# A Toeplitz convolution on TensorE: the zero quarter of each 128x128 tile is left out, with 64x64 tiles for the first halves of chunks and the states, and 128x64 tiles for the second halves

## The chip, the cores and the metric

The kernel runs on one core of a Trainium2 chip. The metric is device time in microseconds (us) of one execution. Names in the text are those of the profile: PE is TensorE's matmuls, PEld its weight loads, DVE is VectorE, ACT is ScalarE, POOL is GpSimd, SP is SyncE, which issues most transfers. L760 is line 760 of the kernel before.

## The reference

The model takes x (64 batches, 64 heads, 1024 positions), runs a masked long convolution per head, and adds a feed-forward layer that is a mixture of 64 experts of rank 16.

```python
mask = (jnp.arange(Lq) < length[:, None]).astype(u.dtype)
u_m = u * mask[:, None, :]
kernel = _get_kernel(log_dt, C, log_A_real, A_imag, Lq)   # K = 2 Re sum_n Cs exp(dtA * l)
n = 2 * Lq
k_f = jnp.fft.rfft(kernel, n=n)
u_f = jnp.fft.rfft(u_m, n=n)
y = jnp.fft.irfft(u_f * k_f, n=n)[..., :Lq]
y = y + u_m * D[:, None]
cond = y * mask[:, None, :]
...
scores = xf @ Wr.T
top_vals, top_idx = jax.lax.top_k(scores, TOPK)
gates = jax.nn.softmax(top_vals, axis=-1)
...
h = jnp.einsum('nd,krd->nkr', xf, A)
out = jnp.einsum('nkr,kdr->nd', h * G[:, :, None], B)
x = x + (out * SCALING).reshape(*prefix, -1)
```

All of it is in 32-bit floats. The convolution of a head is causal: position l of the output takes the positions up to l, with a kernel that is a sum of 64 decaying complex exponentials.

## The kernel before

A sequence of 1024 positions is cut into 8 chunks of 128. Within a chunk the convolution is a product with a 128x128 triangular Toeplitz matrix (`toep`, one per head); what comes from earlier chunks goes through 64 complex states per head. The 64 heads are worked in 8 groups g of 8 heads, a group in 4 pairs i of two heads hh. The work of a group on TensorE is, in order:

- `into_states` (L696 to L712, called by `begin`): per pair and per real or imaginary part c, two products of x with the tables `bt` into the bank `pu`, one head into PSUM partitions 0 to 63 and the other into 64 to 127 (128x64 tiles, 448 columns: 7 chunks of 64 batches). ScalarE copies the bank to the states `s`.
- `recur`: VectorE runs the recurrence over the chunks on `s` (scalar_tensor_tensor, L465 by the helper).
- `inside` (L751, matmul at L760): per head, the Toeplitz tile times x: 128 rows, 128 columns of weights, 512 columns of x (8 chunks of 64 batches) into a bank `pc`.
- `across` (L765, matmul at L769): per pair, per c and per head, 64 state rows times the table `w`, added to columns 64 on of the same bank (64x128 tiles, 448 columns). The head picks the row half of the array.
- L777: VectorE multiplies each `pc` with the mask into `y`, the feature layout that the layer behind reads.

A group runs `inside(0), inside(1), across(0), across(1)` (the names `first_two`), later `inside(2), inside(3), across(2), across(3)` (`last_two`). Between and around them `conv` yields, and products of the group before (L652, the first factor of the experts, by Strassen's seven products at 128x128 with 256 columns) are put in. After `last_two` comes `begin(g + 1)` with the next group's `into_states`, then the gates (`psh`, L849). In group 0 there is little to put in between. The second factor (L1172) runs after the last group, from 606.7 us to the end.

Each 32-bit matmul call is two records of PE and two of PEld in the profile, except transposes. PSUM: `pc` and `pu` share the banks of `ps_k` and `ps_c`, two each, by pair. So the first `pu` after `last_two` needs the bank of pair 2 to be freed by its mask product.

x of a pair (512 KB) is loaded by SyncE (`load_x`, L147) into one of four tiles; the tile is free when `inside` of its last user is done. The Toeplitz tiles are made through DRAM: the first 128 values of each head's kernel (plus D at place 0) are stored to `krows` behind 127 zeros, and one transfer with overlapping rows reads them as a 128x128 tile per head (`rows_by_head`, L333 and L334; `rows` for group 0, L340 and L342). The tables of groups 0 to 3 are made from powers `lv`, those of groups 4 to 7 in transposed form by `tables_as_they_lie`. A planner orders instructions of an engine by the order of the program unless they are not ready in its estimate; where the order is pinned, the code says `keep_in_program_order`.

Of the kernel before, what the change touches and what calls it, by code (L numbers as in the profile page):

```python
# [37 lines left out]
F32 = mybir.dt.float32  # L38
# [6 lines left out]
P = 128  # L45
# [19 lines left out]
NW = P + 1  # L65
# [15 lines left out]
def constants():  # L81


    c = np.zeros((P, NW + P + 2 + NBLK), np.float32)
    c[:, :NW] = np.arange(NW)
    c[:, NW : NW + P] = np.eye(P)
    for hh in range(2):
        c[hh * NS : (hh + 1) * NS, NW + P + hh] = 1.0
    c[:, NW + P + 2 :] = P * np.arange(NBLK)[None, :] + np.arange(P)[:, None]
    return c  # L90


def body(ctx: ExitStack, tc, x, xo, lens, par, dvec, dgrp, at, bm, wt, cst, out):
# [34 lines left out]
    cst_sb = ids.tile([P, NW + P + 2 + NBLK], F32, tag="cst", name="cst_sb")  # L128
# [3 lines left out]
    d_sb = const.tile([2, NP], F32, tag="dvec", name="d_sb")  # L132
    nc.scalar.dma_start(d_sb, dvec)
    d_of_group = const.tile([HG, NG], F32, tag="dgrp", name="d_of_group")
# [4 lines left out]
    feat = cst_sb[:, NW + P + 2 :]  # L139
# [115 lines left out]
    def tables(g):  # L255
# [62 lines left out]
        def kernels_by_vector():  # L318

            kc = tabp.tile([P, HG], F32, tag="kc", name=f"kc_{g}")  # L320
            V.tensor_reduce(kc.rearrange("p (i a) -> p i a", a=2),
# [3 lines left out]
            ks = tabp.tile([HG, P], F32, tag="ks8", name=f"ks8_{g}")  # L325
            nc.scalar.copy(ks, pk)
            return ks

        def rows_by_head(ks):

            tt(ks[:, 0:1], ks[:, 0:1], d_of_group[:, g : g + 1], ALU.add)
            row = krows[h0 : h0 + 1, :]
            nc.sync.dma_start(krows[h0 : h0 + HG, P - 1 :], ks)  # L333
            nc.sync.dma_start(toep, bass.AP(row.tensor, row.offset, [[1, P], [KROW, HG], [1, P]]))  # L334

        def rows(ks, i, n):

            tt(ks[:, :, 0], ks[:, :, 0], d_sb[:, j0 + i : j0 + n], ALU.add)
            row = krows[h0 + 2 * i : h0 + 2 * i + 1, :]
            nc.sync.dma_start(  # L340
                krows[h0 + 2 * i : h0 + 2 * n, P - 1 :].rearrange("(i a) l -> a i l", a=2), ks)
            nc.sync.dma_start(toep[:, 2 * i : 2 * n, :],  # L342
                              bass.AP(row.tensor, row.offset, [[1, P], [KROW, 2 * (n - i)], [1, P]]))

        def tables_as_they_lie():
# [7 lines left out]

            mag, f, lo, k = (flat(t) for t in ("mag", "f", "sn", "k"))
            place = feat[:, 0:1]
# [4 lines left out]
            nc.scalar.activation(mag, mag, AF.Exp, scale=place)  # L360
            ts(f, f, place, ALU.mult)
# [3 lines left out]
            stt(f, lo, place, ALU.mult, f, ALU.add)  # L365
# [41 lines left out]
        for i in range(GP if g < DIRECT else 0):  # L407
            j = j0 + i
            re, im = w[:, 0, i, :P], w[:, 1, i, :P]
# [3 lines left out]
            b = bb[:, i % 2]  # L413
            for c, by in enumerate((alpha, nbeta)):
                if g == 0:
                    ts(b[:, c, :], re, by[:, j : j + 1], ALU.mult)
                else:
                    nc.scalar.activation(b[:, c, :], re, AF.Copy, scale=by[:, j : j + 1])
            stt(b[:, 0, :], im, nbeta[:, j : j + 1], ALU.mult, b[:, 0, :], ALU.add)
            stt(b[:, 1, :], im, nalpha[:, j : j + 1], ALU.mult, b[:, 1, :], ALU.add)  # L420
# [16 lines left out]
        V.tensor_copy(turn[:, 0:2], w[:, :, :, P])  # L437
# [286 lines left out]

    def conv(g, steps, out):
# [13 lines left out]
        def recur(*pairs):  # L739
            for k in range(1, NCH):  # L740
                for i in pairs:
                    s, a = states[i][1], turn[:, 0, i : i + 1]
                    stt(s[:, :, k, :], s[:, :, k - 1, :], a, ALU.mult, s[:, :, k, :], ALU.add)
                for i in pairs:
                    s, b = states[i][1], turn[:, 1, i : i + 1]
                    stt(s[:, 0, k, :], s[:, 1, k - 1, :], b, ALU.mult, s[:, 0, k, :], ALU.add)
                for i in pairs:
                    s, nb = states[i][1], turn[:, 2, i : i + 1]
                    stt(s[:, 1, k, :], s[:, 0, k - 1, :], nb, ALU.mult, s[:, 1, k, :], ALU.add)

        def inside(i):  # L751
            xt, s = states.pop(i)
            pcs = []
            for hh in range(2):
# [653 lines left out]
```

## Time and profile before

| | |
|---|---|
| time, median of 3 runs | 951.28 us (951.0 to 951.71) |
| profiled execution, first to last instruction | 949.7 us; a time of its own is not listed, and 1.6 us lie between it and the median |
| PE busy | 937.7 us (99%), 4232 records |
| PEld busy | 724.9 us |
| DVE busy | 735.8 us (77%) |
| POOL busy | 332.1 us (35%) |
| ACT busy | 160.5 us (17%) |
| inside (L760) | 128 records, 57.7 us of PE |
| across (L769) | 256 records, 53.8 us of PE |
| into the states (L707) | 256 records, 50.5 us of PE |

A row of a group of instructions gives line, engine, operation, output <- input, partitions x elements of both, count, then busy time in us and the mean duration of one in ns, then the idle time of the engine just before them and what ended it. The ends of matmuls are modelled and overlap the next one, so the sum of durations is more than the busy time. A row of the timeline begins with the start and the length of a merged stretch in us from the span's start; in a stretch table a line gives the stretch, its length, the busy time asked for, the TensorE clock granted (1.00 is full speed), the share of the 16 DMA engines' time in use and GB/s.

### The profile page before, as it was taken

The numbers are of one execution on the slowest core, as the hardware profiler recorded it, in microseconds if no ns is written. First come the engines' busy times: TensorE is split into PE (matmuls) and PEld (weight loads), VectorE is DVE, ScalarE is ACT, GpSimd is POOL, SyncE is SP. The second block draws the span as 40 slices with busy tenths as digits, with TensorE's granted clock in tenths as the row PEclk, the third lists the DMA queues.
The fourth block names the chain that finished last, engine by engine and source line by source line (L and its number), as shares of the span: only waits on it lengthen the run. The fifth ranks groups of instructions, "written<-read, shape, count | busy, mean of one in ns | idle before, by whom it ended". The sixth has DMA issues, their size and how long they took to land. (4 is left out here: it accounts for less than half of the span.)

```text
span 949.7 us, 11906 instructions
## 1 busy us (share of the span) xinstructions
PE 937.7 (99%) x4232; PEld 724.9 (76%) x4232; DVE 735.8 (77%) x1717; ACT 160.5 (17%) x292; POOL 332.1 (35%) x285
## 2 busy tenths in 40 slices
PE   7999999999999999999999999999999999999998
PEld 2476767587587587587587688888888888888887
DVE  8899798697995995995893498869856865785674
ACT  5343233312402402411210000000000000000000
POOL 0203204043042041041142032256745554764565
PEclk9999999999999999999999999999999999999999
DMA  8815325237444434334332374663682575258332
GB/s 289 220 44 179 106 85 170 101 102 215 123 127 167 122 119 162 136 108 157 118 106 89 127 253 164 217 236 107 218 283 88 177 263 180 92 208 306 103 123 100
DMA packets 72043, 149.32 MB, mean 157 GB/s; under 512 B 9808, under 2 KB 20784, under 8 KB 71984
## 3 DMA queue, kind: packets, MB, share of 16 engines
q1 hardware_dynamic: 52300, 99.65, 31.8%
q0 software_dynamic: 16864, 47.22, 15.3%
q10 hardware_dynamic: 2820, 1.69, 0.6%
q8 instruction: 33, 0.54, 0.2%
q14 instruction: 26, 0.21, 0.1%
HBM read 100.13 MB, written 47.33 MB: 155 GB/s over the span
## 5 line engine op out<-in xcount | busy, mean ns | idle before, releaser
L465 DVE SCALAR_TENSOR_TENSOR s<-s,turn 128x64 f32<-128x64 f32 (+1 forms) x432 | 119.4, 324 | 2.7 <-ACT s L712 2.0
L652 PE MATMUL h<-y,waa 128*128 128x256 f32 x512 | 117.9, 381 | 0.0
L652 PE MATMUL h<-y,was 128*128 128x256 f32 x512 | 116.5, 380 | 0.0
L652 PE MATMUL h<-ty,was 128*128 128x256 f32 x512 | 116.0, 380 | 0.0
L934 POOL TENSOR_TENSOR hg<-h_p,gx 128x512 f32<-128x512 f32 x16 | 26.8, 1678 | 242.8 <-DVE h_p L465 238.1
L652 PEld LDWEIGHTS h<-y,waa 128*128 128x128 f32 x512 | 96.2, 190 | 19.0 <-issue 6.5
L652 PEld LDWEIGHTS h<-y,was 128*128 128x128 f32 x512 | 97.0, 190 | 14.8 <-issue 1.5
L652 PEld LDWEIGHTS h<-ty,was 128*128 128x128 f32 x512 | 97.3, 190 | 13.7 <-DVE f L465 0.8
L934 POOL TENSOR_TENSOR hg<-h_u,gx 128x512 f32<-128x512 f32 x32 | 48.6, 1519 | 74.5 <-DVE h_u L454 48.3
L1186 ACT COPY p<-s 128x512 f32<-128x512 f32 x28 | 16.4, 586 | 312.4 <-PE s L1172 312.4
L1031 POOL TENSOR_TENSOR o<-o,acc_a 128x512 f32<-128x512 f32 x32 | 47.6, 1506 | 41.4 <-DMA r<-hg_dram 21.7
L652 PE MATMUL h<-ty,waa 128*128 128x256 f32 x256 | 58.4, 382 | 0.0
L760 PE MATMUL pc<-x,toep 128*128 128x512 f32 x128 | 57.7, 594 | 0.6 <-DVE y L777 0.6
L777 DVE TENSOR_TENSOR y<-pc,mask 128x512 f32<-128x512 f32 x64 | 40.7, 682 | 21.4 <-PE pc L769 21.3
L652 PEld LDWEIGHTS h<-ty,waa 128*128 128x128 f32 x256 | 48.3, 190 | 9.5 <-issue 2.0
L454 DVE TENSOR_TENSOR o<-o,s 128x512 f32<-128x512 f32 x50 | 34.1, 682 | 23.5 <-PE s L1172 17.9
L1031 POOL TENSOR_TENSOR o<-o,b_room 128x512 f32<-128x512 f32 x32 | 48.7, 1542 | 9.8 <-DVE b_room L454 9.8
L907 POOL DMA_DIRECT2D gx<-gt_dram x56 | 33.8, 618 | 50.9 <-DMA gt_dram<-gt 50.9
L707 PE MATMUL pu<-x,bt 128*64 128x448 f32 x256 | 50.5, 544 | 0.0
L937 POOL DMA_DIRECT2D hg_dram<-hg x32 | 25.6, 801 | 69.5 <-DVE hg L454 44.5
L1031 POOL TENSOR_TENSOR o<-o,u 128x512 f32<-128x512 f32 x36 | 45.8, 1298 | 10.0 <-DVE u L454 9.7
L454 DVE TENSOR_TENSOR hg<-hg 128x512 f32<-128x512 f32 x64 | 42.4, 681 | 4.7 <-POOL hg L934 4.3
(270 smaller groups left out, 1645.6 us busy)
## 6 DMA issues: line engine op xcount, KB each, us to landing
x<-in_x SPq DMA_DIRECT2D x32, 512.0 KB
hg_dram<-hg POOLq DMA_DIRECT2D x16, 1024.0 KB, 6.0
o<-in_xo SPq DMA_DIRECT2D x64, 256.0 KB
out<-o SPq DMA_DIRECT2D x63, 256.0 KB
gx<-gt_dram POOLq DMA_DIRECT2D x56, 256.0 KB, 4.9
qy<-hg_dram SPq DMA_DIRECT2D x28, 512.0 KB
r<-hg_dram SPq DMA_DIRECT2D x26, 512.0 KB
hg_dram<-hg POOLq DMA_DIRECT2D x16, 768.0 KB, 4.2
```

The lines of the kernel that those rows point to most:

```text
L454: V.tensor_tensor(out=o, in0=a, in1=b, op=o_)
L465: V.scalar_tensor_tensor(out=o, in0=a, scalar=s, in1=b, op0=o1, op1=o2)
L652: nc.tensor.matmul(bank[:, ii, :], lhsT=fac[n - 1][:, k, (j + ii) * P : (j + ii + 1) * P], rhs=rf[n - 1][:, k, :], start=(first and ii == ...
L707: nc.tensor.matmul(pu[hh * NS : (hh + 1) * NS, :], lhsT=bt[:, i, (1 - c) * P + hh * NS : (1 - c) * P + (hh + 1) * NS], rhs=xt[:, hh, : NCH ...
L760: nc.tensor.matmul(pc, lhsT=toep[:, 2 * i + hh, :], rhs=xt[:, hh, :], start=True, stop=False)
L777: marks["y"] = V.tensor_tensor(out=y[:, :, i // 2, 2 * (i % 2) + hh, :], in0=pcs[hh].rearrange("p (k b) -> p k b", b=NB), in1=mask, op=ALU ...
L907: i = queue.dma_start(gx[:, ii, :], gt_dram[g, c * n : (c + 1) * n, :].unsqueeze(1).to_broadcast([n, RANK, TOK]),)
L934: G.tensor_tensor(out=o, in0=a, in1=b, op=op)
L937: nc.gpsimd.dma_start(hg_dram[g, :, a:b, j : j + 2, :], hg[:, a:b])
L1031: tc.keep_in_program_order(G.tensor_tensor(out=o, in0=a, in1=b, op=op_))
L1186: nc.scalar.copy(p1, c11)
```

## The change

A lower triangular 128x128 tile has a 64x64 quarter that is zero. The change doesn't multiply it:

- The first 64 outputs of a chunk come from its first 64 inputs alone (`early_halves`): 64x64 tiles with 256 columns, 4 chunks at a time. The last 64 come from all 128 inputs (`late_halves`): 128x64 tiles with 256 columns.
- The head hh of a pair now picks the row half in which the first 64 inputs lie: x and the Toeplitz tiles of the even heads have their two halves exchanged. The even chunks (e = 0) and the odd chunks (e = 1) are put apart in x, in the states and in the banks, and the odd chunks' outputs have their halves exchanged (`half_of`), so that the four early products of a pair lie on four different 64x64 quarters of the array.
- `across` is also cut into 64x64 tiles: per pair, c and e, four products with the same four quarters; 192 columns for e = 0 (its first chunk has no state before it) and 256 for e = 1. So there are 16 calls per pair instead of 4.
- The order becomes `early_halves` of two pairs, `across` of both, `late_halves` of both. The mask product and the release of the x tile stand behind the late halves.
- The rows of the Toeplitz tile go through three stores and three loads instead of one and one, and D is added at a place that depends on the head.
- The tables get two segments of 65 powers, in an order that depends on the head (131 columns instead of 129), and the transposed tables of groups 4 to 7 do three of their operations per head half. The mask's positions, x, A and Wr are permuted on their way in, to the new order of y's features.

```diff
-NW = P + 1
+HP = P // 2
+SEG = HP + 1
+NW = 2 * SEG + 1
...
+    c = np.zeros((P, NW + P + 2 + NBLK + 1), np.float32)
+    for hh in range(2):
+        for seg in range(2):
+            late = seg == hh
+            c[hh * NS : (hh + 1) * NS, seg * SEG : (seg + 1) * SEG] = HP * late + np.arange(SEG)
+    c[:, NW - 1] = P
...
+def places():
+
+
+    t, p = np.arange(NBLK)[None, :], np.arange(P)[:, None]
+    odd = t // KH
+    return P * (2 * (t % KH) + odd) + (p + HP * odd) % P
...
+        def load_toeplitz(i, n):
+
+
+            row = krows[h0 + 2 * i : h0 + 2 * i + 1, :]
+            heads_of = toep[:, 2 * i : 2 * n, :].rearrange("p (i a) c -> p a i c", a=2)
+
+            def load(o, count, start):
+                nc.sync.dma_start(
+                    o, bass.AP(row.tensor, row.offset + start, [[1, count], [2 * KROW, n - i], [1, P]]))
+
+            load(heads_of[:, 1], P, KROW)
+            load(heads_of[:HP, 0], HP, HP)
+            load(heads_of[HP:, 0], HP, 0)
+
         def rows_by_head(ks):
 
-            tt(ks[:, 0:1], ks[:, 0:1], d_of_group[:, g : g + 1], ALU.add)
-            row = krows[h0 : h0 + 1, :]
-            nc.sync.dma_start(krows[h0 : h0 + HG, P - 1 :], ks)
-            nc.sync.dma_start(toep, bass.AP(row.tensor, row.offset, [[1, P], [KROW, HG], [1, P]]))
+            first = ks.rearrange("h (s j) -> h s j", s=2)[:, :, 0]
+            tt(first, first, d_of_group[:, g, :], ALU.add)
+            dst = krows[h0 : h0 + HG, P - 1 :].rearrange("(i a) l -> a i l", a=2)
+            nc.sync.dma_start(dst[1], ks[GP:])
+            nc.sync.dma_start(dst[0, :, HP:], ks[:GP, :HP])
+            nc.sync.dma_start(dst[0, :, :HP], ks[:GP, HP:])
+            load_toeplitz(0, GP)
...
+            def of_heads(t, hh):
+                return t.rearrange("p (i a n) -> p a i n", a=2, n=NS)[:, hh]
+
             mag, f, lo, k = (flat(t) for t in ("mag", "f", "sn", "k"))
-            place = feat[:, 0:1]
             row(f, 1)
             row(mag, 0)
             row(lo, 2)
             yield
-            nc.scalar.activation(mag, mag, AF.Exp, scale=place)
-            ts(f, f, place, ALU.mult)
+            for hh in range(2):
+                nc.scalar.activation(of_heads(mag, hh), of_heads(mag, hh), AF.Exp, scale=place_of[hh])
+            for hh in range(2):
+                ts(of_heads(f, hh), of_heads(f, hh), place_of[hh], ALU.mult)
             ts(k, f, MAGIC, ALU.add, MAGIC, ALU.subtract)
             yield
             tt(f, f, k, ALU.subtract)
-            stt(f, lo, place, ALU.mult, f, ALU.add)
+            for hh in range(2):
+                stt(of_heads(f, hh), of_heads(lo, hh), place_of[hh], ALU.mult, of_heads(f, hh), ALU.add)
...
         for i in range(GP if g < DIRECT else 0):
             j = j0 + i
-            re, im = w[:, 0, i, :P], w[:, 1, i, :P]
+            re, im = (w[:, c, i, : 2 * SEG].rearrange("p (s j) -> p s j", s=2)[:, :, :HP]
+                      for c in range(2))
...
+    def of_chunk(k):
+
+        return k // 2 + KH * (k % 2)
+
...
         def recur(*pairs):
             for k in range(1, NCH):
+                now, was = of_chunk(k), of_chunk(k - 1)
                 for i in pairs:
                     s, a = states[i][1], turn[:, 0, i : i + 1]
-                    stt(s[:, :, k, :], s[:, :, k - 1, :], a, ALU.mult, s[:, :, k, :], ALU.add)
+                    stt(s[:, :, now, :], s[:, :, was, :], a, ALU.mult, s[:, :, now, :], ALU.add)
                 for i in pairs:
                     s, b = states[i][1], turn[:, 1, i : i + 1]
-                    stt(s[:, 0, k, :], s[:, 1, k - 1, :], b, ALU.mult, s[:, 0, k, :], ALU.add)
+                    stt(s[:, 0, now, :], s[:, 1, was, :], b, ALU.mult, s[:, 0, now, :], ALU.add)
                 for i in pairs:
                     s, nb = states[i][1], turn[:, 2, i : i + 1]
-                    stt(s[:, 1, k, :], s[:, 0, k - 1, :], nb, ALU.mult, s[:, 1, k, :], ALU.add)
...
-        def inside(i):
-            xt, s = states.pop(i)
-            pcs = []
-            for hh in range(2):
-                if g == 0:
-                    banks, tag = ((ps_c, "pc"), (ps_f, "pf"))[i % 2]
-                else:
-                    banks, tag = ((ps_k, "pk"), (ps_c, "pc"))[i % 2]
-                pc = banks.tile([P, NBLK * NB], F32, tag=tag, name=f"pc_{g}_{i}_{hh}")
-                nc.tensor.matmul(pc, lhsT=toep[:, 2 * i + hh, :], rhs=xt[:, hh, :],
-                                 start=True, stop=False)
-                pcs.append(pc)
-            return i, s, pcs
-
-        def across(i, s, pcs, pinned=False):
+                    stt(s[:, 1, now, :], s[:, 0, was, :], nb, ALU.mult, s[:, 1, now, :], ALU.add)
+
+        def half_of(e, late):
+
+            c = (e ^ late) * HP
+            return slice(c, c + HP)
+
+        def chunks(e):
+            return slice(e * KH * NB, (e + 1) * KH * NB)
+
+        def early_halves(*pairs):
+
+
+            made = []
+            for i in pairs:
+                xt, s = states.pop(i)
+                pcs = []
+                for hh in range(2):
+                    if g == 0:
+                        banks, tag = ((ps_c, "pc"), (ps_f, "pf"))[i % 2]
+                    else:
+                        banks, tag = ((ps_k, "pk"), (ps_c, "pc"))[i % 2]
+                    pcs.append(banks.tile([P, NBLK * NB], F32, tag=tag, name=f"pc_{g}_{i}_{hh}"))
+                for e in range(2):
+                    for hh in range(2):
+                        r = slice(hh * HP, (hh + 1) * HP)
+                        nc.tensor.matmul(
+                            pcs[hh][half_of(e, 0), chunks(e)], lhsT=toep[r, 2 * i + hh, :HP],
+                            rhs=xt[r, hh, chunks(e)], start=True, stop=False, skip_group_check=True)
+                made.append((i, xt, s, pcs))
+            return made
+
+        def across(i, xt, s, pcs, pinned=False):
             for c in range(2):
+                for e in range(2):
+                    into, of = ((slice(NB, KH * NB), slice(KH, NCH)), (chunks(1), slice(0, KH)))[e]
+                    for hh in range(2):
+                        o = hh * NS
+                        for late in range(2):
+                            seg = SEG * (hh if late else 1 - hh) + 1
+                            m = nc.tensor.matmul(
+                                pcs[hh][half_of(e, late), into], lhsT=w[o : o + NS, c, i, seg : seg + HP],
+                                rhs=s[o : o + NS, c, of].rearrange("p k b -> p (k b)"),
+                                start=False, stop=False, skip_group_check=True,
+                            )
+                            if pinned:
+                                tc.keep_in_program_order(m)
+
+        def late_halves(i, xt, s, pcs):
+            for e in range(2):
                 for hh in range(2):
-                    o = hh * NS
-                    m = nc.tensor.matmul(
-                        pcs[hh][:, NB:], lhsT=w[o : o + NS, c, i, 1:],
-                        rhs=s[o : o + NS, c].rearrange("p k b -> p (k b)"),
-                        start=False, stop=(c == 1),
-                    )
-                    if pinned:
-                        tc.keep_in_program_order(m)
+                    nc.tensor.matmul(
+                        pcs[hh][half_of(e, 1), chunks(e)], lhsT=toep[:, 2 * i + hh, HP:],
+                        rhs=xt[:, hh, chunks(e)], start=False, stop=(e == 1), skip_group_check=True)
             for hh in range(2):
                 marks["y"] = V.tensor_tensor(
                     out=y[:, :, i // 2, 2 * (i % 2) + hh, :],
...
-        first_two = inside(0), inside(1)
+        first_two = early_halves(0, 1)
         across(*first_two[0])
         across(*first_two[1])
+        late_halves(*first_two[0])
+        late_halves(*first_two[1])
...
-        last_two = inside(2), inside(3)
+        last_two = early_halves(2, 3)
         across(*last_two[0])
         across(*last_two[1])
+        late_halves(*last_two[0])
+        late_halves(*last_two[1])
         step(1)
         if g + 1 < NG:
             begin(g + 1)
...
+    turned = np.concatenate([xr[:, HP:], xr[:, :HP]], 1)
+    xc = np.where((np.arange(NH) % 2 == 0)[:, None, None, None], turned, xr)
+    xc = xc.reshape(NH, P, KH, 2, NB).transpose(0, 1, 3, 2, 4)
+    dh = np.zeros((2, NP, 2), np.float32)
+    for hh in range(2):
+        dh[hh, :, 1 - hh] = D.reshape(NP, 2)[:, hh]
+    place = places()
     arrays = {
-        "x": xr.reshape(NH, P, NBLK * NB),
+        "x": xc.reshape(NH, P, NBLK * NB),
 
...
-        "at": A.reshape(NE * RANK, NBLK, P).transpose(2, 1, 0),
+        "dvec": dh,
+        "dgrp": dh.reshape(2, NG, GP, 2).transpose(0, 2, 1, 3).reshape(HG, NG, 2),
+        "at": A.reshape(NE * RANK, L).T[place],
...
-        "wt": Wr.reshape(NE, NBLK, P).transpose(2, 1, 0),
+        "wt": Wr.T[place],
```

## The prediction

> **What bounds the kernel now.** First the busy shares, then the chain of waits:
>
> ```profile
> PE 937.7 (99%) x4232; PEld 724.9 (76%) x4232; DVE 735.8 (77%) x1717; ACT 160.5 (17%) x292; POOL 332.1 (35%) x285
> ...
> PE s L1172 35%; PE h L652 7%; PE psh L849 0%; PE last L1172 0%; DVE ey L1007 0%; DVE acc_a L454 0%; PE psc L859 0%; DVE o L454 0%; DVE e L990 0%; DVEq L454 0%
> ```
>
> TensorE is busy for 937.7 of 949.7 us, and almost all of the rest is the start, where it waits for loads. Every other engine has a fifth of its time free or more. So a microsecond taken from TensorE is a microsecond of the kernel, as long as nothing that TensorE then reaches sooner is late. The groups of TensorE instructions say how much lies in the part that changes:
>
> ```profile
> L760 PE MATMUL pc<-x,toep 128*128 128x512 f32 x128 | 57.7, 594 | 0.6 <-DVE y L777 0.6
> L769 PE MATMUL pc<-s,w 64*128 64x448 f32 x192 | 40.4, 554 | 0.0
> L769 PE MATMUL pc<-s_more,w 64*128 64x448 f32 x64 | 13.4, 537 | 0.0
> ```
>
> That is 57.7 us inside the chunks and 53.8 out of the states. Each call leaves two records (64 calls, 128 records), one after the other on the same tile of the array. The mean duration of a record overlaps with its neighbours, so prices come from the distance between starts. The timeline of TensorE around the second half of one group's convolution:
>
> ```profile
> 302.64 3.62 PE L652 MATMUL h<-y,was 128*128 128x256 f32 x16
> 306.09 3.62 PE L652 MATMUL h<-y,waa 128*128 128x256 f32 x16
> ...
> 313.00 3.60 PE L760 MATMUL pc<-x,toep 128*128 128x512 f32 x8
> 316.52 1.78 PE L769 MATMUL pc<-s,w 64*128 64x448 f32 x8
> 318.13 1.67 PE L769 MATMUL pc<-s_more,w 64*128 64x448 f32 x8
> 319.73 6.24 PE L707 MATMUL pu<-x,bt 128*64 128x448 f32 x32
> ```
>
> Sixteen records of 256 columns take 3.45 us: 0.216 us for a pass of 256 columns over the whole array. The weight loads of the same stretch show what half tiles do:
>
> ```profile
> 316.52 0.30 PEld L769 LDWEIGHTS pc<-s,w 64*128 64x128 f32 x4 [0.76 <-issue]
> 317.00 0.20 PEld L769 LDWEIGHTS pc<-s,w 64*128 64x128 f32 x2 [0.18 <-issue]
> 317.38 0.19 PEld L769 LDWEIGHTS pc<-s,w 64*128 64x128 f32 x2 [0.18 <-issue]
> 317.75 0.19 PEld L769 LDWEIGHTS pc<-s_more,w 64*128 64x128 f32 x2 [0.18 <-issue]
> ```
>
> They come two at a time, a pair each 0.375 us, so the two row halves run side by side at 448 columns. L707 does the same with column halves: 32 records in 6.06 us, 0.375 a pair and 0.06 at the start. By length, 192 columns take 0.162.
>
> **What a change of tile shape costs.** The last L760 start is at 316.00 and L769 starts at 316.52: 0.09 more than the 0.43 between 512-column records. L769's first pair then takes 0.48 instead of 0.375, another 0.10 while the 128-column weights come in; on going to 64-column weights this is 0.05 (L707: 319.73 to 320.16).
>
> **The change on TensorE, for two head pairs** (half of a group's convolution; `first_two` or `last_two`).
> Before: 8 records of 0.431 inside, 8 pairs of 0.375 across: 3.45 + 3.00 = 6.45 us. Shape changes: in and out of 64x128, 0.38 where products (128x128) follow, 0.34 where L707 (128x64) follows. 6.83 and 6.79.
> After, if four 64x64 tiles run at once: early halves, two records on each of four tiles per pair of heads, 2 x 2 x 0.216 = 0.86. Across, per pair and per c two rounds of 192 and two of 256 columns: 2 x 0.162 + 2 x 0.216 = 0.755, x 4 = 3.02; the same work as before in four times the instructions. Late halves, four records on each of two column tiles per pair: 2 x 4 x 0.216 = 1.72. Sum 5.60. Changes of shape: into 64x64 0.14, into 128x64 0.14, back to 128x128 0.19; but L707 follows the late halves in the same shape and costs nothing. 6.07 and 5.88.
> So the first half of a group gains 0.76 us and the second 0.91: 1.67 a group, 11.7 us over groups 1 to 7.
>
> The trace has no four tiles at once. Its bounds are the rows with two: all four (both the row halves of L769 and the column halves of L707 show no loss) or only two. I take four, since each pair of the four is one of these two combinations. In the late halves the second column tile's work stands behind four records of the first, where the trace shows it passing two; if it can pass no more, one pass of 0.216 is lost per half, 3.0 us in all. I take 0 and keep 3.0 for the range.
>
> That the tiles run ahead of each other is seen at the head of the stage. The two records of a call stand one behind the other for one tile, and the second of one tile has to wait 0.375 us for the first; still two start before 316.8, so one of them is the other head's:
>
> ```profile
> 316.52 0.65 PE L769 MATMUL pc<-s,w 64*128 64x448 f32 x2
> ```
>
> [...]
>
> **What comes earlier and may be late.**
> (1) x. A tile of x is free only after its late half, no more after L760. SyncE's queue shows the two loads of 512 KB for the next group:
>
> ```profile
> 314.91 2.09 SPq L147 DMA_DIRECT2D x<-in_x  x2
> ```
>
> They are issued at 1.92 and 3.63 us after the half's start at 313.00, 0.2 after their L760 records. After the change, pair 2's late half ends at 0.14 + 0.86 + 3.02 + 0.14 + 0.86 = 5.02 and pair 3's at 5.88: issues at 5.2 and 6.1. L707 begins at 5.88 and needs pair 2's x after two pairs of 1.50, at 8.9, and pair 3's at 10.4. And the DMA engines are fullest just there:
>
> ```profile
> 318.00:319.00 1.00, 1.00 0.84 176
> 319.00:320.00 1.00, 1.00 0.99 258
> 320.00:321.00 1.00, 1.00 1.02 379
> 321.00:322.00 1.00, 1.00 1.03 424
> ```
>
> The table (stretch, length, clock, DMA share, GB/s) shows a 1 MB store of hg from POOL that overlaps. The page has no landing time for x; the nearest rows are
>
> ```profile
> hg_dram<-hg POOLq DMA_DIRECT2D x16, 1024.0 KB, 6.0
> ...
> gx<-gt_dram POOLq DMA_DIRECT2D x56, 256.0 KB, 4.9
> ...
> hg_dram<-hg POOLq DMA_DIRECT2D x16, 768.0 KB, 4.2
> ```
>
> From 4.2 to 6.0 us, the second pair's x lands at 9.4 to 11.2: TensorE waits 0.5 to 2.3 at each border between groups; a wait there delays the need of pair 3 as well. The borders into groups 4 to 7 are of this kind; into 2 and 3 there are 1.46 us of transposes and products between (L707 starts 8.20 after the half), which leaves 0 to 0.9 each; into group 1 there are over 25 us. I take 0.5 x 4 = 2.0 us, as that store is issued at 316.73, 1.5 us ahead of where the first load then comes; bounds 0 and 2.3 x 4 + 0.9 x 2 = 11.0.
> (2) y. L707's first bank is freed by the mask product of pair 2, which begins at 318.49 because VectorE is busy until then; it ends 6.2 after the start, against 5.9. These 0.3 lie within the 0.5.
> (3) VectorE is 55 to 62 us busy in 72 us of a group. Per group from 4 on it gets one more tensor_scalar and one scalar_tensor_tensor and ScalarE one activation, on halves (0.69 us for the full width, so some 0.1 each of overhead); tables of 131 instead of 129 columns add 0.01 an operation. The 10 free microseconds hide this; without them it would be under 2 us. TensorE coming 0.9 earlier to products that wait for VectorE's bank releases: 0.2 in all.
> (4) Toeplitz rows. Three stores and three loads instead of one and one: four more issues of 0.3 to 0.37 on SyncE's queue. For groups 2 on the load is issued at 334.15 and needed at 364.5; in group 1 at 79.23 and 90.83. Hidden. x and row loads behind them on the queue wait for TensorE anyway.
> (5) Group 0. TensorE waits there: 33.53 + 3.28 ends L769, and L760 starts at 37.36 after y and after the second toep load (issued 31.75). Early halves finish sooner but then wait for the recurrence; late halves finish y 0 to 0.5 later, and the toep load starts up to 1 us later. Gain 0, between -0.8 (gain) and +1.5.
> (6) The last group's end waits for y of pair 3, whose four mask products take 2.6 us from the end of late half 2: 0.25 of the gain lost.
>
> **Sum.** -11.7 + 2.0 + 0.2 + 0.25 + 0 = -9.2 us. The profiled execution's span is 949.7, and 1.6 us lie around it up to the median of 951.3 (runs 951.0 to 951.7), which do not change. 951.3 - 9.2 = 942.1.
>
> **The rivals.**
> A, four tiles, but only two of them work at a time, because issue follows program order or a port is shared. For: no row shows more than two. Against: both pairings show no loss. Early 1.72, across 6.04, late 1.72, changes 0.47: 9.95 us a half against 6.83, about +3.05 x 14 = +43: 994 us, slower. It decides from the point where the 64x64 part, 3.88 us, grows by 0.84: fewer than 3.3 tiles at once on average.
> B, x late by the full 6.0 us (the full DMA engines speak for it, the short store against): 951.3 - 11.7 + 0.45 + 11.0 = 951.0, no change. With landings above 6.2 us it is slower.
> C, the late halves of the two columns run one after the other: +1.72 x 14 = 24 us, 966; L707's column halves speak against it.
>
> **How the numbers follow.** Likeliest 0.71, its own range 938.4 (no waits for x, group 0 gains) to 948. A 0.13, C 0.02. B and what lies between it and the likeliest 0.14, half of it within 0.2% (1.9 us, about what a measurement of this kernel can tell from no change), the rest split evenly. The range 938 to 953 leaves out A, C and a little on both sides. Faster 0.74, same 0.07, slower 0.19.
>
> **What would show it.** L760's groups: 64x64 records of 256 columns, four weight loads together and a start of four each 0.216 us. A half's convolution 6.0 instead of 6.8 us. L707 beginning 5.9 after the half's start, with an idle time in front of its third pair that ends with a DMA x<-in_x, 0.5 us or so. VectorE's and POOL's busy times unchanged within 3 us. Wrong if the four weight loads come in two pairs, if the across part takes longer than 3.1 us, or if L707 waits for more than 1 us.

## The result: 967.3 us, slower by 1.7%

The changed kernel takes 967.33 us (median of four runs, 965.0 to 969.8), the kernel before 951.21 beside it: a ratio of 1.0167, interval 1.0148 to 1.0186. The profiled execution has a span of 964.6 us against 949.7. The lines that answer to those shown of before, from the page of the changed kernel (busy shares, then the chain of waits by engine and by line):

```profile
PE 936.2 (97%) x5384; PEld 746.0 (77%) x5384; DVE 741.2 (77%) x1725; ACT 151.2 (16%) x288; POOL 332.4 (34%) x285
...
PE 88%; DVE 8%; DMA 3%; issue 1%; ACT 0%; DVEq 0%
PE h L692 38%; PE s L1252 34%; PE pu L747 4%; PE pc L834 4%; PE psh L929 3%; DMA x<-in_x 3%; PE pc L845 2%; DVE s L505 1%; PE pc L820 1%; DVE bt L494 1%; DVE hg L494 1%; DVE f L494 1%; DVE f L505 0%; DVE y L849 0%; PE psc L939 0%
```

TensorE's share fell from 99% to 97%, and `DMA x<-in_x` stands in the chain with 3% of the span. The chain shown of before reaches over 43% of its span only, so it can't settle that this is new; the waits can: in the kernel before TensorE has no wait for x in front of the into-the-states products. The timeline of TensorE around the border into group 4 (start and length in us, then the group, and what the idle time ahead ended with):

```profile
242.05 1.09 PE L820 MATMUL pc<-x,toep 64*64 64x256 f32 x16
242.96 1.69 PE L834 MATMUL pc<-s,w 64*64 64x192 f32 x32
244.48 1.69 PE L834 MATMUL pc<-s_more,w 64*64 64x192 f32 x32
246.10 2.00 PE L845 MATMUL pc<-x,toep 128*64 128x256 f32 x16
248.22 3.23 PE L747 MATMUL pu<-x,bt 128*64 128x448 f32 x16
255.13 5.87 PE L747 MATMUL pu<-x,bt 128*64 128x448 f32 x16 [3.67 <-DMA x<-in_x]
260.81 1.47 PE L929 MATMUL psh<-y,wt_sb 128*64 128x512 f32 x6
```

The half's convolution is as forecast: early halves 0.91 us, across 3.14, late halves 2.12 here and 1.93 elsewhere. The loss is in the two lines behind it. L747 does pairs 0 and 1, waits 3.67 us for pair 2's x, and then takes 5.68 us for sixteen records that took 3.0 just before. The waits of TensorE by cause (total, times, longest):

```profile
PE pu L747 <- DMA x<-in_x: 12.3, 4, 4.0
PE pc L820 <- DMA toep<-krows: 3.2, 1, 3.2
```

The stretch table says why the second sixteen are slow (stretch, length, then busy time and instructions of PE, PEld, DVE, ACT and POOL, the granted clock, the DMA share, GB/s):

```profile
251.15:255.13 3.98, 0.31 (x3) 0.04 (x1) 3.87 (x18) 0.66 (x2) 0.00 (x0) 0.81 0.85 274
255.13:260.81 5.68, 5.68 (x17) 2.08 (x19) 4.31 (x20) 1.60 (x3) 0.00 (x0) 0.53 0.03 12
260.81:264.24 3.43, 3.43 (x18) 1.09 (x14) 1.13 (x5) 0.53 (x1) 0.00 (x0) 1.00 0.00 0
```

TensorE's granted clock falls to one half at 253.65 us, in the middle of this idle time, and stays there after x has landed: the half clock lasts to 260.48, that is 6.8 us; at the border into group 5 it is 6.8 us again, at the border into group 6 it is 3.4. What of it lies on work costs 2.7, 3.0 and 1.7 us.

Added up over TensorE's timeline, from the start of one kind of product to the start of the next, the two profiled executions differ like this (us):

| part | before | after | difference | forecast |
|---|---|---|---|---|
| convolution, groups 1 to 7 (14 halves) | 94.3 | 84.3 | -10.0 | -11.7, with the next row |
| products of the first factor, groups 1 to 7 | 368.5 | 369.4 | +0.9 | |
| into the states, at seven borders | 42.7 | 63.8 | +21.0 | +2.0 |
| up to the end of group 0 | 56.7 | 59.7 | +3.0 | 0 |
| everything else | | | +0.1 | +0.45 |
| span | 949.65 | 964.64 | +15.0 | -9.2 |

Of the 21.0, waits for x are 12.3 and the half clock is 7.4. The last question of the profile is why x came so late. SyncE's queue at this border, in the changed kernel:

```profile
248.80 0.34 SPq L385 DMA_DIRECT2D rf<-rows_of  x1
249.23 0.90 SPq L163 DMA_DIRECT2D x<-in_x  x2
```

and in the kernel before:

```profile
242.74 2.09 SPq L147 DMA_DIRECT2D x<-in_x  x2
247.62 0.34 SPq L351 DMA_DIRECT2D rf<-rows_of  x1
```

The planner has put the first row load of the next tables (`rf`) ahead of the loads of x for pairs 2 and 3, since these are now free later. The row load itself waits: its tile is last read by ScalarE's second sine, which runs from 248.15 to 248.77. So x of pair 2, free after its late half at about 247.2, is issued at 249.23, 7.2 us after the half's start instead of the 5.2 of the forecast. The same stands at the borders into groups 5 and 6. At the border into group 7, in the same kernel, no row load stands ahead: x of pair 2 is issued at 479.36, 5.2 us after the half's start at 474.14, its products begin at 483.98, and what TensorE waits for there is ScalarE (0.69 us), not x.

### The profile page after: what moved, and what is told of

It is laid out like the page before. It is cut to its first block, busy times and chain, and to the rows that moved or that the text cites. A ratio compares the mean times of both kernels' runs of the same rounds, so it can differ in the third digit from the quotient of the medians.

```text
span 964.6 us, 14262 instructions
## 1 busy us (share of the span) xinstructions
PE 936.2 (97%) x5384; PEld 746.0 (77%) x5384; DVE 741.2 (77%) x1725; ACT 151.2 (16%) x288; POOL 332.4 (34%) x285
## 4 chain that ended last, share of the span: by engine, by line
PE 88%; DVE 8%; DMA 3%; issue 1%; ACT 0%; DVEq 0%
PE h L692 38%; PE s L1252 34%; PE pu L747 4%; PE pc L834 4%; PE psh L929 3%; DMA x<-in_x 3%; PE pc L845 2%; DVE s L505 1%; PE pc L820 1%; DVE bt L494 1%; DVE hg L494 1%; DVE f L494 1%; DVE f L505 0%; DVE y L849 0%; PE psc L939 0%
## 5 line engine op out<-in xcount | busy, mean ns | idle before, releaser
L747 PE MATMUL pu<-x,bt 128*64 128x448 f32 x256 | 58.6, 608 | 13.4 <-DMA x<-in_x 12.3
L747 PEld LDWEIGHTS pu<-x,bt 128*64 128x64 f32 x256 | 19.5, 150 | 48.2 <-issue 32.6
L505 DVE SCALAR_TENSOR_TENSOR s_more<-s_more,turn 128x128 f32<-128x128 f32 x144 | 45.9, 319 | 5.6 <-ACT s_more L752 5.6
```

Of the source, the lines that this page charges most:

```text
L505: V.scalar_tensor_tensor(out=o, in0=a, scalar=s, in1=b, op0=o1, op1=o2)
L747: nc.tensor.matmul(pu[hh * NS : (hh + 1) * NS, :], lhsT=bt[:, i, (1 - c) * P + hh * NS : (1 - c) * P + (hh + 1) * NS], rhs=xt[:, hh, : NCH ...
```

## The experiments

Theory T: x is released late, the row load delays it further on SyncE's queue, and the idle time halves TensorE's clock; the half tiles themselves are as fast as forecast. Rival R: the time is lost in the 64x64 work, its four times longer instruction stream or the permuted tables. Line numbers are those of each kernel; every time is a median beside runs of the kernel before on the same chip (951.0 to 951.2). The ratios and their intervals are taken over the runs, so the quotient of the medians can differ from them by up to 0.2%.

**1. The late release without half tiles.** The kernel before in its own tiles, with `across` ahead of `inside` in every half (the last half is shown; `across` now starts the bank, and the mask products stand behind `inside`):

```diff
-        last_two = inside(2), inside(3)
+        last_two = banks_of(2), banks_of(3)
         across(*last_two[0])
         across(*last_two[1])
+        inside(*last_two[0])
+        inside(*last_two[1])
```

> The kernel before, in its own tiles (128x128 inside, 64x128 across) and with its own tables, but with the order across, then inside in every half of a group: only the place where x is freed changes, to about 4.7 and 6.5 us after the half's start, close to where the changed kernel frees it (5.0 and 5.9). Theory T: waits of TensorE for x of some 3 to 5 us at the borders into groups 4 to 6 and half clock after them, some 10 to 20 us in all: 960 to 972 with no 64x64 tile in it. Rival R (the loss comes from the half tiles or their tables): 949 to 953, as before.

Measured: 977.90 us, ratio 1.0272 (1.0232 to 1.0311). SyncE's queue, then TensorE's timeline, at the border into group 4:

```profile
255.12 0.34 SPq L351 DMA_DIRECT2D rf<-rows_of  x1
255.97 0.34 SPq L351 DMA_DIRECT2D rsn<-rows_of  x1
256.43 0.90 SPq L147 DMA_DIRECT2D x<-in_x  x2
```

```profile
251.62 3.70 PE L764 MATMUL pc<-x,toep 128*128 128x512 f32 x8
256.48 3.53 PE L707 MATMUL pu<-x,bt 128*64 128x448 f32 x16 [1.16 <-DVE y L767]
263.12 3.23 PE L707 MATMUL pu<-x,bt 128*64 128x448 f32 x16 [3.11 <-DMA x<-in_x]
```

More than T had said, and without one 64x64 tile: row loads move ahead of x, and TensorE waits for x, 9.6 us in all. About 18.5 us of the loss lie at the borders; 6.5 lie in group 0, where TensorE waits 3.7 us for a mask product and 1.0 for the recurrence. Not all of the 18.5 is x: the mask products are later here too, and TensorE waits 3.5 us for them at three borders. R has no place for this.

**2. The row load out of the way.** In the changed kernel the row loads are issued on POOL's queue:

```diff
             def row(t, n):
-                nc.sync.dma_start(
+                G.dma_start(
                     t, rows_of[n, j0 : j0 + GP, :].rearrange("j q -> (j q)").partition_broadcast(P))
```

> The changed kernel with one thing moved: the loads of the three parameter rows of groups 4 to 7 are issued on POOL's queue instead of SyncE's, so no row load can stand ahead of the x loads of pairs 2 and 3. Theory T with its parts apart: the load of x for pair 2 is issued about 5.2 us after the half's start instead of 7.1; if that block is the main part, TensorE waits 1 to 2 us less at each of the borders into groups 4, 5 and 6, the idle time falls to 1 to 2 us, the clock is not halved, and the time is 948 to 956. If the late release alone is enough for a wait that halves the clock, 960 to 966. Rival R: 965 to 970.

Measured: 955.40 us, ratio 1.0035 (1.0020 to 1.0050). SyncE's queue, then TensorE, at the same border:

```profile
250.28 1.72 SPq L163 DMA_DIRECT2D x<-in_x  x2
```

```profile
245.06 1.09 PE L820 MATMUL pc<-x,toep 64*64 64x256 f32 x16
...
251.83 3.23 PE L747 MATMUL pu<-x,bt 128*64 128x448 f32 x16 [0.72 <-DVE y L849]
256.18 3.23 PE L747 MATMUL pu<-x,bt 128*64 128x448 f32 x16 [1.12 <-DMA x<-in_x]
```

The load is issued 5.2 us after the half's start, to the tenth the estimate of the prediction; TensorE still waits 1.1 to 1.7 us at each of four borders (5.2 in all), and the clock stays whole there (1.00 from 245 to 265 us; the sixteen records behind the wait take 3.0 us at the borders into groups 4 to 6). From issue to use x takes 5.9 us here too. So 12 us of the loss, by the medians, are the row load's place and the half clock that the longer wait brought on. Between the two profiled executions it is 13.8 us at the borders, while group 0 cost 6.0 us in this execution, against 3.0 in the changed kernel's: more on that below.

**3. The idle time filled, nothing else touched.** The gates' products are put between pairs 1 and 2 of the into-the-states stage; `begin` now does pairs 0 and 1 and returns a function for pairs 2 and 3, which the gates call (`rest_of`):

```diff
         nc.scalar.copy(sh.rearrange("e (t p) -> e t p", t=NTT), phalf.rearrange("e (p t) -> e t p", t=NTT))
+        if rest_of:
+            rest_of.pop()()
```

> The changed kernel with the gates' 16 products (psh, 3.53 us, of the same 128x64 shape) put between the into-the-states products of pairs 1 and 2 instead of behind those of pair 3. Late release of x, the row load ahead of the x loads, landings, tiles and all operations stay; only the 3.3 to 4.0 us in which TensorE stood idle at the borders into groups 4 to 6 are filled. Theory T (idle time there, and the half clock that follows it, are the loss): waits under 1 us, no half clock, 967.3 - 3 x (3.5 + 3.2) = 947, between 944 and 951. If the half clock comes from something other than the idle time, the stages stay at half speed and it is 956 or more. Rival R (the 64x64 work): 965 to 970.

Measured: 948.43 us, ratio 0.9971 (0.9962 to 0.9980): faster than the kernel before. SyncE's queue still has the row load ahead of x, at 247.91, and x at 248.34. TensorE's timeline:

```profile
247.34 3.23 PE L747 MATMUL pu<-x,bt 128*64 128x448 f32 x16 [0.56 <-DVE y L855]
250.40 3.60 PE L935 MATMUL psh<-y,wt_sb 128*64 128x512 f32 x16
254.81 3.23 PE L747 MATMUL pu<-x,bt 128*64 128x448 f32 x16 [0.81 <-DMA x<-in_x]
```

x is used 6.5 us after its issue, later than in the changed kernel (5.9), but TensorE has been idle for 0.81 us instead of 3.67, and the second sixteen take 3.16 us at full clock. That takes 18.9 us off the changed kernel. With the half tiles, their instructions and tables all in place, R is out; and at the borders the half clock went with the idle time: the granted clock is 1.00 in this whole execution.

**4. Other work in the gap, taken from ahead of the half.** One step of the first factor's products is moved from before `last_two` to behind it:

```diff
         yield
-        yield
         last_two = early_halves(2, 3)
...
         step(1)
+        yield
         if g + 1 < NG:
             begin(g + 1)
```

> The changed kernel with one step of the first factor's products (3.45 or 6.9 us of TensorE) moved from ahead of the second half's convolution to behind it, ahead of the next group's into-the-states stage. Release of x, queue order and all operations stay; only TensorE has other work while x lands. Theory T: the waits for x (3.3 to 4.0 us in a row at the borders into groups 4 to 6) are covered, no half clock there: 946 to 953. It loses where the change of tile shape that the late halves share with the into-the-states stage comes back (0.3 us a group). Rival R: 965 to 970.

Measured: 961.87 us, ratio 1.0104 (1.0069 to 1.0139), a miss. The timeline and SyncE's queue at the border into group 4:

```profile
244.54 3.72 PE L692 MATMUL h<-ty,was 128*128 128x256 f32 x16
248.19 3.23 PE L747 MATMUL pu<-x,bt 128*64 128x448 f32 x16
254.65 4.92 PE L747 MATMUL pu<-x,bt 128*64 128x448 f32 x16 [3.24 <-DMA x<-in_x]
```

```profile
248.17 0.34 SPq L385 DMA_DIRECT2D rf<-rows_of  x1
248.60 0.90 SPq L163 DMA_DIRECT2D x<-in_x  x2
```

The half came 3.5 us earlier, but x only 0.6: it is not TensorE that sets the issue here but the row load, and that waits for ScalarE's sine (247.52 to 248.14 in this kernel), which follows VectorE's work on the tables. So the gap was filled and opened again. It also says what the expectation had overlooked: moving the release earlier is worth nothing while something else stands ahead in the queue.

**5. Late halves ahead of across.** x is then free after 2.1 and 2.9 us (every half is changed in this way, the last is shown; the mask products move behind `across`):

```diff
-        across(*last_two[0])
-        across(*last_two[1])
         late_halves(*last_two[0])
         late_halves(*last_two[1])
+        across(*last_two[0])
+        across(*last_two[1])
```

> The changed kernel with the order early halves, late halves, across in every half of a group; the mask products stand behind across. An x tile is then free about 2.1 and 2.9 us after the half's start instead of 5.0 and 5.9; all the products and their tiles stay. The price is one more change of tile shape per half, about 0.14 us, 2 us in all. Theory T (the changed kernel is slower because x is released late, a row load stands ahead of the x loads on SyncE's queue, and TensorE's clock is halved after the waits): no wait of TensorE for x at the borders between groups, no stretch at half clock there, into-the-states stages of 6.1 us again instead of up to 13.2; some 3 us of group 0's loss stay. 951.2 - 10.6 + 2 + 3 = 945, between 942 and 949. Rival R (the time is lost in the 64x64 work, the longer instruction stream or the permuted tables): 965 to 970, as the changed kernel.

Measured: 953.57 us (949.5 to 954.5), ratio 1.0008 (0.9990 to 1.0026), outside T's range. At the borders T's picture is right: no wait for x but one of 0.9 us, all stages but the last 6.06 to 6.16 us, no half clock. From the end of group 0 on this execution gains 5.6 us on the kernel before. But group 0 costs 8.5, not 3. TensorE's timeline there:

```profile
33.47 1.99 PE L820 MATMUL pc<-x,toep 64*64 64x256 f32 x16 [3.52 <-DMA toep<-krows]
35.39 3.73 PE L849 MATMUL pc<-x,toep 128*64 128x256 f32 x16
...
45.62 5.41 PE L692 MATMUL h<-y,waa 128*128 128x256 f32 x16 [2.27 <-DVE y L842]
```

After each of these waits the clock is halved, for 6.8 and 3.4 us. In the changed kernel the first wait is 3.22 us and no half clock follows. So group 0 became the second question: why do the Toeplitz tiles come late there?

**6. Group 0: the Toeplitz loads.** Theory T0: the three loads of a half (in the changed kernel they land at 29.5, 33.2 and 34.9 us, the single one of before at 28.7) share the DMA engines with POOL's two accumulating loads (in the changed kernel issued at 24.3 and 25.2 us and landing at 32.0 and 35.1; the DMA share there is 1.03 to 1.18 from 29 to 34 us). These are moved behind the landing of the second half, in the kernel of experiment 5, in the kernel before as a control, and in the kernel of experiment 3 (what the texts call the first experiment is experiment 5 here):

```diff
-    behind_landing(x_tiles[6][0:1, 1, 0:1])
-    third_sum(wa_quarters[0])
...
             behind_landing(toep[0:1, HG - 1, 0:1])
+            third_sum(wa_quarters[0])
             fourth_sum(wa[2], wa[5])
```

> The late-halves-first order of the first experiment, and POOL's two accumulating loads of group 0 (was<-in_at, issued at 23 and 24 us, landing at 29 and 33) moved behind the landing of the second half of the Toeplitz tiles, in front of the four loads that already stand there. Theory T0 (group 0 loses because the six small Toeplitz loads share the DMA engines with these accumulating loads and land at 33 to 34 instead of 29, after which TensorE's clock is halved): the idle time of 3.5 us ahead of the first early halves falls below 1 us, no half clock there, 953.6 - 7 = 946, between 942 and 949. Rival (the six transfers are slow by themselves, as rows of 64 short pieces): 951 to 955, as without it.

> The kernel before with POOL's two accumulating loads of group 0 moved in the same way: the control for that move. Its first Toeplitz load lands at 28.7 us, ahead of its use at 29.9, and the second is waited for by 0.6 us at most, so T0 expects 950.3 to 951.6, no change. If the move were a gain of its own it would be 948 or less.

> The gates between pairs 1 and 2, and POOL's two accumulating loads of group 0 later as well, in the changed kernel's own order (late halves last, so without the extra change of tile shape of 2 us in all). If T and T0 hold, both costs go and the convolution's gain of 10.6 us stays but for waits under 1 us at a border: 951.2 - 10.6 + 1 to 3 = 941.6 to 944. If T0 falls: 947, as the gates between alone.

Measured: 951.08 us, ratio 0.9996 (0.9987 to 1.0005); the control 951.05, 0.9998 (0.9989 to 1.0008); gates between 948.62, 0.9973 (0.9962 to 0.9983), the same as without the move. The control is as expected, the other two are misses. The wait for the Toeplitz tiles is gone in both, as T0 says, and the first products with those tiles begin at 29.97 and 29.91 us, but a wait for a mask product stands in its place. With the gates between:

```profile
29.91 1.09 PE L824 MATMUL pc<-x,toep 64*64 64x256 f32 x16
...
39.97 1.70 PE L824 MATMUL pc<-x,toep 64*64 64x256 f32 x16 [3.13 <-DVE y L853]
41.76 5.26 PE L690 MATMUL h<-y,waa 128*128 128x256 f32 x16
```

VectorE's timeline of the same kernel shows where those mask products stand, in the middle of the recurrence of pairs 2 and 3, although the late halves had ended at 36.8, and how idle VectorE is behind them:

```profile
39.24 2.47 DVE L853 TENSOR_TENSOR y<-pc,mask 128x512 f32<-128x512 f32 x4
...
51.28 1.29 DVE L853 TENSOR_TENSOR y<-pc,mask 128x512 f32<-128x512 f32 x2 [8.53 <-PE pc L849]
```

In the kernel before they begin at 35.96. So T0 is right on the loads and wrong on the time: two waits lay over each other in group 0.

**7. Group 0: the mask products earlier.** On top of gates between and the later loads, `recur(2, 3)` is cut after its fourth step and the rest is issued behind the mask products:

```diff
-            late_halves(*first_two[0])
-            late_halves(*first_two[1])
-            recur(2, 3)
+            late_halves(*first_two[0], False)
+            late_halves(*first_two[1], False)
+            recur(2, 3, steps_=range(1, 5))
+            for i, _, _, pcs in first_two:
+                masked(i, pcs)
+            with tc.issue_after(marks["y"].ins):
+                recur(2, 3, steps_=range(5, NCH))
```

> The last kernel (gates between, POOL's loads later) with one change in group 0: VectorE's four mask products of pairs 0 and 1 stand behind the fourth of the seven steps of the recurrence of pairs 2 and 3 instead of behind the fifth and a bit (39.24 us there), so at about 36.4 to 37.5 us. Theory V (with the Toeplitz wait gone, group 0 waits 3.1 us for these mask products because of their place in VectorE's order, and the products behind run at half clock for 1.7 us): the wait falls below 1 us, no half clock, 948.6 - 2.3 - 1.7 = 944.6, between 943 and 946.5. Rival (something else, the second Toeplitz load or the recurrence, ends last there): 947 to 949.

> The same with the row loads of groups 4 to 7 on POOL's queue, so that the x loads of pairs 2 and 3 are issued about 2 us earlier. If the gates' products cover the late x fully, this changes nothing: within 1 us of the kernel without it. If what is left of the waits for x (0.8 us in all in the gates-between kernel) and the tight borders cost more than that, it is 1 to 2 us faster.

Measured: 946.66 us, ratio 0.9952 (0.9939 to 0.9964), just outside V's range, and with the row loads on POOL's queue too 944.35, ratio 0.9937 (0.9924 to 0.9951). The wait in group 0 is 1.57 us instead of 3.13, with no half clock behind in the profiled execution; 2.0 us gained of the 4.0 expected. The row loads are worth another 2.3 between the medians, but the two intervals overlap, and part of it is luck: the first median is a run with a mean granted clock of 0.998, the second one with 1.000. Between the two profiled executions, both at whole clock, it is 1.5 us, and the waits at the borders that were left (0.8 us for x, 0.8 for a mask product) are gone. The border into group 4 of this last kernel, the fastest of all:

```profile
243.12 2.00 PE L855 MATMUL pc<-x,toep 128*64 128x256 f32 x16
245.25 3.23 PE L745 MATMUL pu<-x,bt 128*64 128x448 f32 x16
248.30 3.60 PE L942 MATMUL psh<-y,wt_sb 128*64 128x512 f32 x16
251.74 3.33 PE L745 MATMUL pu<-x,bt 128*64 128x448 f32 x16
```

No wait is left there. Its span is 7.2 us below that of before; group 0 is still 1.2 us longer than before.

**8. Is it the half tiles?** The kernel before with the same moves (gates between, loads later, row loads on POOL's queue):

> The control for the moves: the kernel before, with its full tiles, and with the gates' products between pairs 1 and 2 of the into-the-states stage, POOL's accumulating loads of group 0 later and the row loads on POOL's queue (all but the mask products' place in group 0, which it has early by itself). It has no waits for x at the borders, so under T these moves remove nothing: 950 to 952. If they shorten it by several us, the best kernel's 944.4 is not the half tiles' doing.

Measured: 951.74 us, ratio 1.0003 (0.9992 to 1.0014). The moves are worth nothing by themselves; what makes 944.35 is the work that the half tiles save. (The earlier mask products are not in this control; in the kernel before they begin at 35.96 us as it is.)

## Why the prediction was wrong, point by point

- **Four tiles at once: right.** A half of a group takes 5.98 us up to the products that follow, 6.07 in the prediction; across 3.14 against 3.02 plus its share of the shape changes, late halves 1.93. Rivals A and C did not occur. The convolution saved 10.0 us and gave 0.9 back in the products behind; the forecast of 11.7 was 2.6 too much: 0.9 for the way back to 128x128, and the rest in the second halves. At the borders with L747 right behind three of four gained 0.56 us (6.73 to 6.17) and not 0.91; in groups 1, 2 and 7 other products follow, and 0.75 is gained.
- **Step (1), x: wrong, and the step that decided.** "issues at 5.2 and 6.1" is right for a queue with nothing else in it: experiment 2 measured 5.2, and so did the border into group 7. The row load that now stood ahead made it 7.2. From issue to use it then took 5.9 us where the estimate had taken 4.2, near the upper end of its bounds. The wait was 3.3 to 4.0 us at three borders and 1.2 at a fourth, 12.3 us in all instead of 2.0, already outside its upper bound of 11.0.
- **Step (4), "x and row loads behind them on the queue wait for TensorE anyway": the sentence that failed.** It looked at what the new Toeplitz transfers delay, and did not ask which other load, due between the old and the new time of x, would pass it. Experiment 2 prices the row load's place, with the half clock that it brought on, at 12 us.
- **What was left out: the clock.** Every wait was priced at its length. The half clock behind the waits added 7.4 us. It lasted 6.8, 6.8 and 3.4 us at the three borders, and in experiment 5 an idle time of 2.27 us was enough for 3.4 us of it (last section). The prediction had allowed for waits of up to 2.3 us at a border and did not ask what one of 3 or 4 us does.
- **Step (5), group 0: sized wrong.** Gain 0 with bounds of -0.8 and +1.5; measured +3.0. Of the three loads the last landed at 34.9 us, 6.2 later than the one load had (28.7), while POOL's accumulating loads ran beside them up to 35.1 (with these moved, in experiment 6, no wait for the tiles is left), and the mask products moved from 35.96 to 39.3 in VectorE's order. The second alone does it: with the loads out of the way, group 0 still costs 4.5 us in experiment 6, its half clock included. The first alone was not run.
- **Steps (2), (3) and (6): small, as forecast.** y costs 0.2 us at the border into group 4, where L747 begins at 248.22, right behind the mask product that ends at 248.17; VectorE is busy for 741.2 us against 735.8, a little more than the 3 us allowed.
- **Rival B was the right mechanism** (x late by about 6 us), with a price of no change since its issue was taken at 5.2 us and the clock as whole. Its "With landings above 6.2 us it is slower" counted the landing alone: the kernel is slower with 5.9. With the waits covered by other work, experiment 7 comes to 944.35, 2.2 us from the forecast of 942.1; that is another kernel, and does not make the forecast right for this one.
- **The range's lower end** of 938.4 is 0.9 us below what its terms give: 942.1 - 2.0 - 0.8 = 939.3.

## What to carry to other kernels

When a change frees a buffer later, go through the queue that refills it and list every other transfer that becomes due between the old and the new time: it may now stand ahead, and wait for yet another engine. Don't price a wait of TensorE at its length alone: most of those of 2.3 to 4.3 us in these runs had the half clock behind them, for 3.4 or 6.8 us, and each 3.4 us of it costs up to 1.7 us. And where a release can't be earlier, put work that needs nothing of it between the release and the use; taking that work from ahead of the release only helps if the release is what the transfer waits for.

## What was unexpected in the hardware

In these runs the half clock lasted 3.4 or 6.8 us, and the length of an idle time does not say which. 3.57 us brought none (group 0 of experiment 3, mean granted clock 1.000), 3.67 us brought 6.8 us in the changed kernel and less in experiment 4 (border into group 5: the sixteen records behind the wait take 4.63 us there and 5.87 in the changed kernel, against 3.23 at whole clock), and the 2.27 us of experiment 5 brought 3.4. Nor is its start tied to the idle time: it lay 2.2 and 3.1 us into the idle times of 3.67 and 4.05 us, and after one of 3.24 us (experiment 4) it came 1 us after TensorE had started again (at 255.66, with the start at 254.65).

The trace's record of the granted clock shows what it went with. In the changed kernel the half clock begins at 253.65, 332.16 and 410.66 us and ends at 260.48, 338.98 and 414.08: stretches of 6.83, 6.83 and 3.41 us, with 71.68 us at whole clock between them, 2, 2, 1 and 21 times 3.413 us. Cut into pieces of this length, TensorE's time looks like this (stretch, length, then PE's busy time, the granted clock, DMA share, GB/s; first the idle time of 3.22 us in group 0, then the borders into groups 4 and 6, all in the changed kernel, and last the 2.27 us of experiment 5):

```profile
28.37:31.79 3.42, 1.68 (x10) 1.00 1.04 199
31.79:35.20 3.41, 1.93 (x40) 1.00 0.85 158
...
250.24:253.65 3.41, 1.21 (x8) 1.00 0.71 201
253.65:257.07 3.42, 1.94 (x6) 0.50 0.42 161
257.07:260.48 3.41, 3.41 (x12) 0.50 0.02 5
...
407.25:410.66 3.41, 0.08 (x3) 1.00 0.93 294
410.66:414.08 3.42, 3.42 (x10) 0.50 0.04 17
...
42.69:46.10 3.41, 1.14 (x17) 1.00 1.02 332
46.10:49.52 3.42, 3.42 (x10) 0.50 1.04 204
```

In what was measured here the half clock goes with the busy time of the piece before. At whole clock, pieces with 1.21, 0.27 and 0.08 us busy are followed by half clock in the changed kernel, and those of 1.68 and 1.93 in its group 0 are not. Cut in the same way from where their half clock begins, experiments 5 and 6 have pieces with 1.14 and 1.54 us busy that are followed by it, and experiment 1 has one of 1.66 that is not. At half clock, 1.94 and 2.50 us busy are followed by another half piece in the changed kernel, 3.41 by the whole clock, and 2.73 by the whole clock in experiment 1. So the idle time of 3.22 us that fell across two pieces cost its length alone, and the one of 2.27 us inside a single piece 1.7 us more. No run moved the pieces by themselves, so this is read off a few traces, is not the result of an experiment and sets no limit; busy times go by modelled ends of matmuls.

The spread between runs goes with the granted clock. In the last kernel of experiment 7 three runs with a mean granted clock of 1.000 take 944.2 to 944.4 us, and two with 0.998, which answers to one piece at half clock, 945.8 and 946.1. The changed kernel, at 0.989 to 0.994, spreads over 4.8 us. The runs of the kernel before that stand beside it spread over 0.7, but among those beside the experiments there are some of 954.4 to 957.5 us, at 0.996 to 0.998.
